# Rounding weight pieces on GpSimd instead of ScalarE, and copies ahead of an exponential, in a gated cross-attention and quantised FFN kernel

## The chip, the cores and the metric

The kernel runs on one core of a Trainium2 chip. The metric is the device time of one execution in microseconds (us). The engines are named PE (TensorE, matrix products), DVE (VectorE), ACT (ScalarE), POOL (GpSimd) and SP (SyncE, which here only starts transfers). Each engine takes its instructions in order, from its own queue.

## The reference

Two layers are computed one after the other, each added to its input through a tanh gate:

```python
x = x + tanh(g_xattn) * xattn(layernorm(x), ctx, Wq, bq, Wk, bk)
x = x + tanh(g_ffn)   * ffn(layernorm(x), w_gate, w_up, w_down)

def xattn(text, features, Wq, bq, Wk, bk):       # text, features (8, 256, 1024)
    Q = text @ Wq.T + bq
    K = features @ Wk.T + bk
    return softmax(Q @ K.T / sqrt(1024)) @ features

def fake_quant(t, axis):                         # one scale per row
    s = max(max(abs(t), axis) / 127, 1e-8)
    return clip(round(t / s), -128, 127) * s

def ffn(x, w_gate, w_up, w_down):                # 1024 -> 2752 -> 1024
    q = fake_quant
    h = silu(q(x) @ q(w_gate).T) * (q(x) @ q(w_up).T)
    return q(h) @ q(w_down).T
```

There are 8 batches of 256 tokens. The three FFN weights have to be quantised row by row: the largest magnitude of a row gives its scale, and each value is divided by the scale and rounded to a whole number.

## The kernel before

**Layout of the work.** The attention does not form Q and K. The kernel first multiplies the two attention weights into one matrix mt (lines 335 to 486), and the scores of a batch are then tokens x mt x features. After that a loop over the batches runs the attention (lines 645 to 695), and the FFN of all batches follows. The FFN weights are quantised during the mt product and the attention loop, in small portions between the attention's steps.

**Order.** From line 164 on to the first nine FFN products everything stands in the order in which the program text issues it ("manual_schedule"), so the text order is the order of each engine's queue. A tile pool with `bufs=n` gives n buffers for a tile's name; the next user of a buffer waits until the earlier user's readers are done.

**Weight pieces (lines 181 to 257).** `pieces` lists 92 portions of [128 rows x up to 1024 columns]: the row blocks of w_gate and w_up (44), and the row blocks of w_down in three column parts, first for the maximum (24) and then again for storing (24). `prepare()` makes one step of a pipeline over this list: it starts the load of piece i on SP (`prepare_load`), finishes piece i-3 (`prepare_store`), and scales piece i-2 (`prepare_scale`). Scaling is DVE's row maximum (L118) and inverse scale (L114), and then GpSimd's `raw * inv + MAGIC` in f32, in place (L209, L221 for w_down); adding MAGIC = 1.5 x 2^23 rounds to a whole number. Finishing is ScalarE's `raw - MAGIC` into the bf16 tile rq (L245, L234), and then a transfer: for w_gate and w_up a transposing DMA on SP into the resident weights (L246), for w_down a store to DRAM from ScalarE's queue (L240). `raw` has four buffers, `rq` has two. The last column part of w_down also gets 64 columns of zeros from ScalarE (L238).

**The attention loop.** Stage b does, in this order:

- `softmax_stage(b)` (L621): scores of the first token tile into a PSUM bank (L526); transposes of the next batch's normalised tokens by PE (L413), a quarter at a time, copied to xT by ScalarE (L436); DVE's shift nm (L534 to L536) and ScalarE's exponential (L542) of the first scores; the first half of the second tile's scores; quarters 2 and 3; one `prepare()`; the rest of the scores; the second shift and exponential.
- `tokens_bias` (L438): two row products on DVE (prod, L441), which write scratch tiles of the same pool name as xq (one buffer).
- `store_steps` (L593): ScalarE's rounding of a token tile of the batch before into xq (L596), and its store.
- eight query products (L508), each 16 matrix products that read all of xT, with ScalarE's copy to H (L512). Between them: transposes of the numerators with the copy pT (L548), the attention products (L555), the residual (L566, DVE, in place in xr), the stores of its rows to DRAM from GpSimd's queue (L667, L674), their statistics (L132), the root (L138, ScalarE, with a table load ahead of it) and inverse (L143 to L148), their normalisation in place (L151) and quantisation (L576), and the same statistics and normalisation for the tokens of the batch after next. `prepare()` stands ten times in a stage.

The token loads (xr, xn) and the feature loads are started on SP, in the same queue as the weight loads and the transposing DMAs.

Of the kernel before, what the change touches and what calls it, by code (L numbers as in the profile page):

```python
# [10 lines left out]
BF16 = mybir.dt.bfloat16  # L11
AF = mybir.ActivationFunctionType
ALU = mybir.AluOpType
# [4 lines left out]
P = 128  # L18


MAGIC = 12582912.0
# [6 lines left out]
def gated_xattn_ffn_kernel(  # L28
# [26 lines left out]
    nc = tc.nc  # L55
    B, S, D = x.shape
# [13 lines left out]
    def rows_of(c):  # L70
        return min(P, FF - c * P)
# [12 lines left out]
    nmagic = const.tile([P, 1], F32, name="nmagic")  # L84
# [15 lines left out]
    def chunk_of(name, c):  # L100
        if c == NFC - 1:
            return resident["tail"][:, :, :TAIL] if name == "wgT" else resident["tail"][:, :, TAIL:]
        t, c = (resident[name, 0], c) if c < CL else (resident[name, 1], c - CL)
        return t[:, :, c * P : (c + 1) * P]
# [5 lines left out]
    def scales(amax, s, tag="inv"):  # L110

        inv = small.tile(list(s.shape), F32, name="inv", tag=tag, bufs=3)
        nc.vector.tensor_scalar(s, amax, 1.0 / QMAX, SMIN, ALU.mult, ALU.max)
        nc.vector.reciprocal(inv, s)  # L114
        return inv

    def abs_max(dst, src):
        nc.vector.tensor_reduce(dst, src, AX.X, ALU.max, apply_absolute_value=True)  # L118
# [36 lines left out]
    def bank(tag):  # L155

        return psum.tile([P, HB], F32, name="ps_" + tag, tag=tag)
# [8 lines left out]
    if True:  # L166
        wraw = keep_scope.enter_context(tc.tile_pool(name="wraw", bufs=4, side=right))
# [13 lines left out]
        for c in range(NFC):  # L181
            pieces += [(w_gate, "wgT", swg, c), (w_up, "wuT", swu, c)]
            for r in range(c * KC // NFC, (c + 1) * KC // NFC):
                pieces += [(w_down, "max", i, r) for i in range(len(down_cols))]
                pieces += [(w_down, "store", i, r) for i in range(len(down_cols))]
        raws, downs = {}, {}
        step = [0]

        def prepare_load(i):
            src, kind, part, r = pieces[i]  # L190
            raws[i] = wraw.tile([P, D], F32, name="raw", tag="raw")
            if src is w_down:
                cols = down_cols[part]
                nc.sync.dma_start(
                    out=raws[i][:, : cols.stop - cols.start], in_=src[r * P : (r + 1) * P, cols]
                )
            else:
                n = rows_of(r)
                nc.sync.dma_start(out=raws[i][:n], in_=src[r * P : r * P + n, :])

        def prepare_scale(i):
            src, kind, part, r = pieces[i]
            raw = raws[i]
            if src is not w_down:
                n = rows_of(r)
                am = small.tile([P, 1], F32, name="wam", tag="wam")
                abs_max(am[:n], raw[:n])
                inv = scales(am[:n], part[:n, r : r + 1])
                nc.gpsimd.tensor_scalar(raw[:n], raw[:n], inv, MAGIC, ALU.mult, ALU.add)  # L209
                return  # L210
            w = down_cols[part].stop - down_cols[part].start
            if kind == "max":
                if part == 0:
                    downs[r] = small.tile([P, len(down_cols)], F32, name="dam", tag="dam")
                abs_max(downs[r][:, part : part + 1], raw[:, :w])
                if part == len(down_cols) - 1:
                    am = small.tile([P, 1], F32, name="wam", tag="wam")
                    nc.vector.tensor_reduce(am, downs[r], AX.X, ALU.max)
                    downs[r] = scales(am, swd[:, r : r + 1], "inv_d")
            else:  # L220
                nc.gpsimd.tensor_scalar(  # L221
                    raw[:, :w], raw[:, :w], downs[r], MAGIC, ALU.mult, ALU.add
                )

        def prepare_store(i):
            src, kind, part, r = pieces[i]
            raw = raws.pop(i)
            if kind == "max":
                return
            rq = wraw.tile([P, D], BF16, name="rq", tag="rq", bufs=2)  # L230
            if src is w_down:
                cols = down_cols[part]
                w = cols.stop - cols.start
                nc.scalar.activation(rq[:, :w], raw[:, :w], AF.Identity, bias=nmagic)  # L234
                if part == len(down_cols) - 1:

                    pad = NFC * P - FF
                    nc.scalar.activation(rq[:, w : w + pad], ones[:, :pad], AF.Identity, scale=0.0)  # L238
                    w += pad
                nc.scalar.dma_start(  # L240
                    out=wdq_dram[r][:, cols.start : cols.start + w], in_=rq[:, :w]
                )
            else:
                n = rows_of(r)
                nc.scalar.activation(rq[:n], raw[:n], AF.Identity, bias=nmagic[:n])  # L245
                nc.sync.dma_start_transpose(out=chunk_of(kind, r), in_=rq[:n])  # L246

        def prepare(n=1):
            for _ in range(n):
                i = step[0]  # L250
                if i < len(pieces):
                    prepare_load(i)
                if 0 <= i - 3 < len(pieces):
                    prepare_store(i - 3)
                if 0 <= i - 2 < len(pieces):
                    prepare_scale(i - 2)
                step[0] += 1
# [136 lines left out]
        for t in range(NTT):  # L394
            nc.sync.dma_start(
                out=x0[t], in_=x[0, t * P : (t + 1) * P, :].rearrange("p (c d) -> p c d", c=2)
# [13 lines left out]
        def transposes(src, blocks):  # L410
            pt = bank("tr").rearrange("p (i t) -> p i t", t=P)
            for i, k in enumerate(blocks):
                nc.tensor.transpose(pt[:, i, :], src[:, k * P : (k + 1) * P], ident)  # L413
            return pt
# [17 lines left out]
        def quarter_transposed(dst, src, g, copy):  # L432

            t, ks = g // 2, range(g % 2 * 4, g % 2 * 4 + 4)
            pt = transposes(src[t], ks)
            copy(dst[:, ks.start : ks.stop, t * P : (t + 1) * P], pt)  # L436
# [10 lines left out]
        cq = {}  # L447
# [76 lines left out]
        def scores(ps, t, js):  # L524
            for j in js:
                nc.tensor.matmul(  # L526
                    ps[:, :L], lhsT=H[:, j, t * P : (t + 1) * P], rhs=fT[:, j, :],
                    start=(j == 0), stop=(j == KC - 1),
                )

        def shift(ps, c):

            nm = small.tile([P, 1], F32, name="nm", tag="nm")
            nc.vector.tensor_reduce(nm, ps[:, :L], AX.X, ALU.max)  # L534
            nc.vector.tensor_scalar(nm, nm, c, -SCALE, ALU.add, ALU.mult)
            nc.vector.scalar_tensor_tensor(nm, c, SCALE, nm, ALU.mult, ALU.add)  # L536
            return nm

        def numerators(ps, nm):
            pe = work.tile([P, L], F32, name="pe", tag="pe")  # L540
            se = small.tile([P, 1], F32, name="se", tag="se")
            nc.scalar.activation(pe, ps[:, :L], AF.Exp, bias=nm, scale=SCALE, accum_out=se)  # L542
            return pe, se
# [77 lines left out]
        def softmax_stage(b, xn):  # L621

            nxt = b + 1 < B
            pss = [bank("s") for _ in range(NTT)]
            scores(pss[0], 0, range(KC))
            if nxt:
                quarter_transposed(xT, xn, 0, nc.scalar.copy)
                quarter_transposed(xT, xn, 1, nc.scalar.copy)
            nums = [numerators(pss[0], shift(pss[0], cq[b][:, 0:1]))]
            scores(pss[1], 1, range(KC // 2))  # L630
            if nxt:
                quarter_transposed(xT, xn, 2, nc.scalar.copy)
                quarter_transposed(xT, xn, 3, nc.scalar.copy)
                prepare()
            scores(pss[1], 1, range(KC // 2, KC))
            nums.append(numerators(pss[1], shift(pss[1], cq[b][:, 1:2])))
            return nums
# [6 lines left out]
        waiting = None  # L644
        for b in range(B - 1):
            nums = softmax_stage(b, xn)
            tokens_bias(b + 1, xn, scratch)
            if waiting:
# [224 lines left out]
    last = (B - 1) * NTT  # L873
    first = {"xq": load_quantised(0), "sx": sx01[:, 0:1, :], "h": []}
    nums = softmax_stage(B - 1, None)
    store_steps(*waiting)
    xr = load_tokens(B - 1, "xr")
    for r in range(KC):
        nc.sync.dma_start_transpose(
            out=wd_early[:, :, r * P : (r + 1) * P], in_=wdq_dram[r][:, : CA * P]  # L880
# [39 lines left out]
    for r in range(KC):  # L920
        nc.sync.dma_start_transpose(
            out=wd_late[:, :, r * P : (r + 1) * P], in_=wdq_dram[r][:, CA * P :]
# [59 lines left out]
    for i in range(2):  # L982
        cols = slice(i * HB // 2, (i + 1) * HB // 2)
# [44 lines left out]
```

## Time and profile before

| | us |
|---|---|
| three runs | 961.87, 964.85, 966.94 |
| their median | 964.85 |
| the profiled execution | 959.2 |
| its span | 957.1 |
| PE busy in it | 934.1 |
| DVE busy | 641.6 |
| ACT busy | 370.0 |
| POOL busy | 149.6 |
| granted PE clock | 1.00 |

The profile shows one execution. The span goes from the first to the last instruction; the profiled execution's own time is 2.1 us longer. Times in a timeline count from the start of the span. A group of instructions is named by its line in the kernel, its engine, its operation, and "out<-in" by tile names. "[1.83 <-ACT xT L436]" behind a row says that the engine had been idle for 1.83 us ahead of it, and that the idle time ended with a write of tile xT by ACT at line 436. In the list of waits the numbers are the total in us, how many times, and the longest. A softmax stage is named here by its b: stage 0 begins at 137 us in the trace, stage 6 at 418 us.

### The profile page before, as it was taken

What the parts mean: (1) busy time and instruction counts of PE and PEld (TensorE: products, weight loads), DVE (VectorE), ACT (ScalarE), POOL (GpSimd) and SP (SyncE); (2) the same over time, 40 slices, a digit from 0 to 9 for tenths busy, and PEclk for the clock granted to TensorE, in tenths of its full rate; (3) what the DMA queues carried; (4) which work ended last, traced back from release to release, by engine and by line L of the source; (5) the groups of instructions that cost most, each with busy time, mean ns of one, the idle gap of its engine ahead of it and who ended that gap; (6) DMA issues with size and microseconds to landing.
All of it is one profiled execution on the core that took longest, in us unless ns stands there. A gap on an engine that the chain in (4) does not pass through costs nothing.

```text
span 957.1 us, 14239 instructions
## 1 busy us (share of the span) xinstructions
PE 934.1 (98%) x5496; PEld 691.3 (72%) x5496; DVE 641.6 (67%) x1326; ACT 370.0 (39%) x660; POOL 149.6 (16%) x153
## 2 busy tenths in 40 slices
PE   9999999999999999999998899999999999999998
PEld 5444687868777878787877776858678586786854
DVE  5977825859585868686367757666576755767673
ACT  0022434445453536454537843423414143241420
POOL 0031311222221221122000003003030020302005
PEclk9999999999999999999999999999999999999999
DMA  9266876969698897967491512012120121201104
GB/s 349 91 170 201 217 237 171 310 214 265 223 241 283 212 288 202 263 208 236 135 204 49 107 23 76 13 23 90 23 89 1 23 89 23 89 1 47 44 1 154
DMA packets 125716, 135.95 MB, mean 142 GB/s; under 512 B 90256, under 2 KB 91536, under 8 KB 125648
## 3 DMA queue, kind: packets, MB, share of 16 engines
q1 hardware_dynamic: 112368, 104.36, 39.5%
q0 software_dynamic: 4784, 16.52, 4.5%
q10 hardware_dynamic: 8496, 14.16, 4.1%
q8 instruction: 43, 0.70, 0.3%
q14 instruction: 25, 0.20, 0.1%
HBM read 87.04 MB, written 26.74 MB: 119 GB/s over the span
## 4 chain that ended last, share of the span: by engine, by line
PE 80%; DVE 11%; ACT 5%; DMA 2%; issue 1%; POOL 0%; ACTq 0%; DVEq 0%
PE ps_g L748 14%; PE ps_tr L748 14%; PE ps_g L508 10%; PE ps_a L841 7%; PE ps_s L841 7%; PE ps_s L508 5%; PE ps_a L555 5%; PE ps_s L313 4%; PE ps_a L313 4%; PE ps_s L526 2%; PE ps_g L313 2%; PE ps_tr L413 2%; DMA wdq_dram<-rq 2%; DVE wam L118 2%; DVE st L132 1%
## 5 line engine op out<-in xcount | busy, mean ns | idle before, releaser
L508 PE MATMUL ps_g<-xT,mt 128*128 128x256 f32 x640 | 145.2, 380 | 4.5 <-ACT xT L436 4.5
L759 ACT ACTIVATE g<-g,swg 128x256 f32<-128x256 f32 (+1 forms) x176 | 79.7, 499 | 158.6 <-DVE g L757 158.6
L508 PEld LDWEIGHTS ps_g<-xT,mt 128*128 128x128 f32 x640 | 119.9, 190 | 25.1 <-ACT xT L436 6.7
L841 PEld LDWEIGHTS <-hq 128*128 128x128 bf16 x726 | 71.4, 98 | 76.0
L861 POOL TENSOR_TENSOR o<-o,xr 128x512 f32<-128x512 f32 x31 | 39.9, 1287 | 392.5 <-DVE o L858 385.5
L769 DVE SCALAR_TENSOR_TENSOR h<-ps_tr,swu,g 128x256 f32<-128x256 f32 x160 | 70.2, 482 | 43.5 <-ACT g L759 41.0
L209 POOL TENSOR_SCALAR raw<-raw,inv 128x1024 f32<-128x1024 f32 (+1 forms) x44 | 54.6, 1241 | 255.1 <-DVE inv L114 144.4
L748 PE MATMUL ps_tr<-xqb,wuT_lo 128*128 128x256 bf16 x704 | 84.7, 273 | 3.5 <-DVE h L769 3.5
L508 PE MATMUL ps_s<-xT,mt 128*128 128x256 f32 x384 | 86.9, 379 | 0.0
L783 DVE TENSOR_TENSOR acc<-acc,g 128x512 f32<-128x512 f32 (+2 forms) x88 | 56.4, 642 | 42.9 <-ACT g L773 42.1
L748 PE MATMUL ps_g<-xqb,wgT_lo 128*128 128x256 bf16 x704 | 84.7, 273 | 0.0
L748 PE MATMUL ps_tr<-xqb,wuT_hi 128*128 128x256 bf16 x640 | 77.7, 273 | 1.3 <-DVE h L769 1.1
L748 PE MATMUL ps_g<-xqb,wgT_hi 128*128 128x256 bf16 x640 | 77.7, 273 | 0.4 <-DVE g L757 0.4
L245 ACT ACTIVATE rq<-raw,nmagic 128x1024 bf16<-128x1024 f32 (+1 forms) x44 | 50.6, 1149 | 70.5 <-POOL raw L209 59.7
L508 PEld LDWEIGHTS ps_s<-xT,mt 128*128 128x128 f32 x384 | 71.2, 190 | 8.7
L748 PEld LDWEIGHTS <-wuT_lo 128*128 128x128 bf16 x704 | 68.9, 98 | 11.8 <-issue 3.8
L748 PEld LDWEIGHTS <-wgT_lo 128*128 128x128 bf16 x704 | 68.9, 98 | 9.9 <-issue 0.6
L826 DVE TENSOR_TENSOR h<-h,bc 128x512 f32<-128x512 f32 x80 | 51.7, 689 | 28.0 <-ACT bc L821 28.0
L748 PEld LDWEIGHTS <-wuT_hi 128*128 128x128 bf16 x640 | 62.6, 98 | 9.1 <-issue 1.8
L748 PEld LDWEIGHTS <-wgT_hi 128*128 128x128 bf16 x640 | 62.6, 98 | 8.0 <-issue 0.7
L566 DVE SCALAR_TENSOR_TENSOR xr<-ps_a,r,xr 128x512 f32<-128x512 f32 x32 | 23.9, 751 | 62.5 <-PE ps_a L555 62.5
L773 ACT ACTIVATE g<-h 128x512 f32<-128x512 f32 x72 | 45.2, 628 | 37.8 <-DVE h L769 37.8
(178 smaller groups left out, 1382.5 us busy)
## 6 DMA issues: line engine op xcount, KB each, us to landing
raw<-in_L_ffn_w_down_dram SPq DMA_DIRECT2D x32, 512.0 KB, 5.7
raw<-in_L_ffn_w_gate_dram SPq DMA_DIRECT2D x21, 512.0 KB, 4.7
raw<-in_L_ffn_w_up_dram SPq DMA_DIRECT2D x21, 512.0 KB, 5.5
fn<-in_ctx_dram SPq DMA_DIRECT2D x8, 1024.0 KB, 6.7
xr<-in_x_dram SPq DMA_DIRECT2D x16, 512.0 KB, 4.5
x_dram<-xr POOLq DMA_DIRECT2D x16, 512.0 KB, 5.2
xr<-x_dram SPq DMA_DIRECT2D x32, 256.0 KB, 3.4
out_dram<-o POOLq DMA_DIRECT2D x31, 256.0 KB, 3.7
```

What stands on the lines that cost most here:

```text
L209: nc.gpsimd.tensor_scalar(raw[:n], raw[:n], inv, MAGIC, ALU.mult, ALU.add)
L245: nc.scalar.activation(rq[:n], raw[:n], AF.Identity, bias=nmagic[:n])
L313: nc.tensor.matmul(pm, lhsT=a[:, c, k * P : (k + 1) * P], rhs=b[:, c, :], start=start, stop=stop)
L508: nc.tensor.matmul(ph, lhsT=mt[:, k, j * P : (j + 1) * P], rhs=xT[:, k, :], start=(k == 0), stop=(k == KC - 1),)
L555: nc.tensor.matmul(pas[h], lhsT=pT[:, l, :], rhs=f_tiles[b][:, l, halves[h]], start=(l == 0), stop=(l == NLT - 1),)
L748: nc.tensor.matmul(pb[:, i, :], lhsT=w[:, k, :], rhs=block["xq"][:, k, :], start=(k == 0), stop=(k == KC - 1),)
L759: nc.scalar.activation(g[:n, i, :], g[:n, i, :], AF.Silu, scale=swg[:n, c : c + 1])
L769: nc.vector.scalar_tensor_tensor(h[:n, i, :], src, swu[:n, c : c + 1], g[:n, i, :], ALU.mult, ALU.mult)
L773: nc.scalar.activation((acc if p == 0 else g)[:n, i, :], h[:n, i, :], AF.Abs)
L783: nc.vector.tensor_tensor(acc[:n, i, :], acc[:n, i, :], g[:n, i, :], ALU.max)
L826: nc.vector.tensor_tensor(h, h, ib.to_broadcast((P, 2, TB)), ALU.mult)
L841: nc.tensor.matmul(pds[t, half][:, cols], lhsT=hq[p][:, i, t * P : (t + 1) * P], rhs=wd[:, half * HB + cols.start : half * HB + cols.stop] ...
```

## The change

The rounding of a weight piece moves from `prepare_store` on ScalarE into `prepare_scale` on GpSimd, straight behind the scaling of the same piece, one step of the pipeline earlier; the bf16 tile rq is kept in a table until the next step stores it. The transfers stay where they were. In `softmax_stage` the exponential of the first token tile is issued behind the copies of quarters 2 and 3; its shift nm stays where it was on DVE.

```diff
@@ def prepare_scale(i):
                 inv = scales(am[:n], part[:n, r : r + 1])
-                nc.gpsimd.tensor_scalar(raw[:n], raw[:n], inv, MAGIC, ALU.mult, ALU.add)
+                rounded(i, raw[:n], inv)
                 return
...
             else:
-                nc.gpsimd.tensor_scalar(
-                    raw[:, :w], raw[:, :w], downs[r], MAGIC, ALU.mult, ALU.add
-                )
+                rounded(i, raw[:, :w], downs[r])
+
+        def rounded(i, raw, inv):
+            rows, cols = raw.shape
+            rq = wraw.tile([P, D], BF16, name="rq", tag="rq", bufs=2)
+            nc.gpsimd.tensor_scalar(raw, raw, inv, MAGIC, ALU.mult, ALU.add)
+            nc.gpsimd.tensor_scalar(rq[:rows, :cols], raw, MAGIC, None, ALU.subtract)
+            rqs[i] = rq
@@ def prepare_store(i):
-            raw = raws.pop(i)
             if kind == "max":
                 return
-            rq = wraw.tile([P, D], BF16, name="rq", tag="rq", bufs=2)
+            rq = rqs.pop(i)
             if src is w_down:
...
-                nc.scalar.activation(rq[:, :w], raw[:, :w], AF.Identity, bias=nmagic)
...
             else:
-                n = rows_of(r)
-                nc.scalar.activation(rq[:n], raw[:n], AF.Identity, bias=nmagic[:n])
-                nc.sync.dma_start_transpose(out=chunk_of(kind, r), in_=rq[:n])
+                nc.sync.dma_start_transpose(out=chunk_of(kind, r), in_=rq[: rows_of(r)])
@@ def softmax_stage(b, xn):
-            nums = [numerators(pss[0], shift(pss[0], cq[b][:, 0:1]))]
+            nm = shift(pss[0], cq[b][:, 0:1])
             scores(pss[1], 1, range(KC // 2))
             if nxt:
                 quarter_transposed(xT, xn, 2, nc.scalar.copy)
                 quarter_transposed(xT, xn, 3, nc.scalar.copy)
+            nums = [numerators(pss[0], nm)]
+            if nxt:
                 prepare()
```

More of the change, by code (lines that the diff above doesn't have):

```diff
@@ L185, in gated_xattn_ffn_kernel @@
                 pieces += [(w_down, "store", i, r) for i in range(len(down_cols))]
-        raws, downs = {}, {}
+        raws, rqs, downs = {}, {}, {}
         step = [0]
```

## The prediction

> **What bounds the kernel now.** I read the page first: busy time by engine, then the chain that ended last.
>
> ```profile
> PE 934.1 (98%) x5496; PEld 691.3 (72%) x5496; DVE 641.6 (67%) x1326; ACT 370.0 (39%) x660; POOL 149.6 (16%) x153
> ...
> PE 80%; DVE 11%; ACT 5%; DMA 2%; issue 1%; POOL 0%; ACTq 0%; DVEq 0%
> ```
>
> TensorE (PE) is busy for 934.1 of 957.1 us. Taking work off ScalarE (ACT, 39%) is worth nothing in itself; only the 23.0 us in which PE idles can be won. So I asked the waits of PE what ends this idleness.
>
> ```profile
> PE ps_g L508 <- ACT xT L436: 4.5, 5, 1.8
> ...
> PE ps_tr L413 <- ACT xT L436: 2.8, 2, 2.1
> ```
>
> Both are PE waiting for ScalarE's copies of the next tokens (xT). The other entries lie in the FFN part and at the ends, which the change does not touch. By windows of 20 us, 0.2 of the 4.5 falls at 107 us, ahead of the softmax stages. The rest, 7.1 us, belongs to five stages: 1.83 in b=1, 1.12 in b=2, 2.07 in b=3, 0.85 + 0.71 in b=4, 0.47 in b=5. Stages 0 and 6 have none. The timeline shows two causes. Stage 1:
>
> ```profile
> 190.71 4.07 POOL L221 TENSOR_SCALAR raw<-raw,inv 128x1024 f32<-128x1024 f32 x3 [14.80 <-DVE inv L114]
> ...
> 191.16 0.67 DVE L536 SCALAR_TENSOR_TENSOR nm<-cq,nm 128x1 f32<-128x1 f32 x1
> ...
> 191.87 0.47 ACT L542 ACTIVATE pe<-ps_s,nm 128x256 f32<-128x256 f32 x1 [3.10 <-DVE nm L536]
> ...
> 192.33 1.06 ACT L436 COPY xT<-ps_tr 128x512 f32<-128x512 f32 x2
> ...
> 192.96 3.72 PE L508 MATMUL ps_g<-xT,mt 128*128 128x256 f32 x16 [1.83 <-ACT xT L436]
> ...
> 194.10 1.75 DVE L441 SCALAR_TENSOR_TENSOR prod<-xn,v_bc 128x1024 bf16<-128x1024 f32 x1
> ...
> 195.90 1.15 ACT L596 ACTIVATE xq<-xr,nmagic 128x1024 bf16<-128x1024 f32 x1 [2.04 <-DVE prod L441]
> ...
> 197.85 0.36 ACT L548 COPY pT<-ps_tr 128x256 f32<-128x256 f32 x1
> ```
>
> The exponential waits for the shift nm, which VectorE (DVE) delivers late; two finished transposes queue behind it on ScalarE, and PE behind them. Stage 3 has the other cause:
>
> ```profile
> 281.86 1.54 POOL L209 TENSOR_SCALAR raw<-raw,inv 128x1024 f32<-128x1024 f32 x1 [3.72 <-issue]
> ...
> 283.43 1.15 ACT L245 ACTIVATE rq<-raw,nmagic 128x1024 bf16<-128x1024 f32 x1 [3.75 <-POOL raw L209]
> ...
> 284.49 1.05 ACT L436 COPY xT<-ps_tr 128x512 f32<-128x512 f32 x2
> ...
> 285.11 1.14 PE L413 MATMUL ps_tr<-ident,xn 128*128 128x128 f32 x8 [2.07 <-ACT xT L436]
> ```
>
> Here the rounding of a weight piece waits for GpSimd (POOL) and holds the first two copies.
>
> **The limit behind it.** In stage 1 the attention product after the next query product needs pT. On ScalarE that copy stands behind xq (L596), which waits for the second prod of VectorE. pT is ready at 197.85 + 0.36 = 198.21 and PE's weight load for the product starts at 199.98: slack 1.77. The same difference is 1.76 in stage 2, 1.30 in 3, 0.52 in 4, 0.51 in 5. VectorE is idle between the last residual (L566) and the prods only while it waits for the square root, so this is a serial chain. If D is how much it grows, a stage gains the smaller of its stall and (slack - D); below zero is a loss.
>
> **The change, part by part.**
>
> *Exponential behind the copies.* Nothing is added. Copies 2 and 3 need only their transposes, which end at 189.40 in stage 1: done by about 190.6, before PE ends its scores at 191.13. The table load (1.28 us, which ran while ScalarE waited) now follows them, to about 191.9, so the exponential runs where it ran before. Its user, the pe transposes behind 3.7 us of query product, has about 2 us to spare. This frees 1.83 + 1.12 + 0.85 + 0.47 = 4.3 us.
>
> *Rounding off ScalarE.* 44 instructions of 1149 ns (50.6 us) and 24 at L234 (18.3 + 7.0 us) leave it: 75.9 us, on an engine that is idle 61%. On the path that is 2.07 + 0.71 us, the stalls of stages 3 and 4. It also helps VectorE's chain:
>
> ```profile
> DVE rr L143 <- ACT rt L138: 9.3, 9, 2.7
> ```
>
> The root waits for a table load that starts after a rounding. With the rounding gone that load starts earlier, and the root is bounded by its input v or by the load: I read 0.4 + 0.7 saved in stage 1, 0.65 in 2, 1.2 in 3, 0.8 in 4, 1.2 in 5. ScalarE keeps the down-weight stores (L240) and the 8 pads (0.24 us each).
>
> *Rounding onto GpSimd.* 68 instructions. No row shows GpSimd writing bf16; the nearest is its scaling of the same tile, 1.12 us at the median. [...] GpSimd then holds about 150 + 68 x 1.12 = 226 us, no bound by itself. What costs is VectorE:
>
> ```profile
> 409.90 1.12 POOL L221 TENSOR_SCALAR raw<-raw,inv 128x1024 f32<-128x1024 f32 x1 [0.55 <-DMA raw<-in_L_ffn_w_down_dram]
> 410.00 1.56 DVE L576 TENSOR_SCALAR xr<-xr,inv 128x1024 f32<-128x1024 f32 x1
> ```
>
> L576 takes 0.753 at the median, so it was held 0.81 and let go at 410.81, 0.21 before GpSimd's recorded end. [...] I place each rounding behind its scaling and see what arrives in its 1.12 us, released 0.2 before its end as in the row:
>
> - Stage 1: nothing. The three scalings at 190.71 already run back to back, and the second prod (1.75 against 1.22) meets the third GpSimd instruction then as it will now. D = -1.1.
> - Stage 2: the root's small products L145 (0.5), L576 (0.16), less 0.65: D = 0.
> - Stage 3: L145 (0.5), L576 twice (0.2, 0.23), L151 of the next tokens (0.47), less 1.2: D = +0.2.
> - Stage 4: L576 twice, L151, and the second prod, as in stage 1 (0.53): 1.43 - 0.8, D = +0.63.
> - Stage 5: L151, L576, prod: 1.23 - 1.2, D = 0.
>
> Gains: 1.83; 1.12; min(2.07, 1.30 - 0.2) = 1.1; 0.52 - 0.63 = -0.1; min(0.47, 0.51) = 0.47. Sum 4.4 us. [...] I take the row, less 0.2 for the weight products at 104.8 (the second prod there, L441, can be held up to 0.8, ahead of mt rows that PE reads some 0.6 later), and less 0.9 for two further blocks of about 0.45 that I can't place. **3.3 us** faster.
>
> *Queues.* The store of a piece stays one step behind, the transposes on SP and the down stores on ScalarE. The rounding needs the rq buffer of two pieces earlier, so its transfer must have landed; that wait moves from ScalarE to GpSimd, one step earlier. Queued behind it there are the next scaling and the stores of the residual rows (L667, L674); VectorE's normalisation of those rows (L151, in place) waits for them. In stage 2 to 3 the store L667 was issued at 254.06. ScalarE's rounding there had waited for a landing until 256.92, so the worst new issue is 256.92 + 1.12 = 258.0; landing takes 5.7 at the median, 263.7, and L151 comes at 268.96: 5.2 us hide it. Without that cover each us late would be a us on VectorE's chain. SP no longer waits for ScalarE's rounding ahead of its transposes; loads are hidden either way (VectorE waits 1.8 us for raw in all), so I count 0.
>
> **The sum.** The profiled execution took 959.2 us, 2.1 beyond its span of 957.1; with 3.3 less it is 955.9. The runs shown have a median of 964.85, 5.65 above it, which I carry over: 964.85 - 3.3 = 961.5 us, 0.34% less.
>
> **The rivals.**
>
> 1. *All stalls go* (blocks on VectorE are fewer, or fall where it waits for PE): 7.1 us less, 957.8. For it: before each residual VectorE waits 2.9 to 5.7 us for PE. Against: those waits lie behind pT, not ahead of it, and stages 4 and 5 have a slack of only 0.5.
> 2. [...]
> 3. *The stall only changes its name*: PE waits for pT as long as it waited for xT, within 1 us of 964.85. For it: the same late VectorE releases both. Against: the slack of 1.77 in stages 1 and 2.
>
> **How the numbers follow.** Chances: forecast (1 to 4.8 us less) 0.42, rival 1 0.25, rival 2 0.20, rival 3 0.13. 0.5% is 4.8 us, about what a measurement of this kernel can tell from no change. Faster by more is rival 1: 0.25. Within it are forecast, rival 3 and a tenth of rival 2: 0.57. Slower by more: 0.18. The range goes from all stalls gone, 957.5, to 969, short of rival 2's 971.5; that leaves out about 2 in 10. The forecast's own range is 960 to 964.
>
> **What would show it.** PE's waits for xT should fall from 7.3 us to below 1. New PE waits for pT at L555 would be VectorE's chain, in stages 3 to 5 first. [...] The waits for the root should fall below 5 us. The forecast fails if PE waits for pT in stages 1 and 2, or if a residual store lands after its normalisation would start.

## The result, and the profile after

The changed kernel takes 963.46 us (median of 14 runs), against 963.57 us for the kernel before, measured beside it: a ratio of 0.9991, 95% interval 0.9972 to 1.0009. No change can be measured. The profiled execution took 961.49 us with a span of 959.4. A later comparison (e11, below) gave 0.9998 (0.9986 to 1.0011).

The page of the changed kernel: busy time by engine, and the chain that ended last.

```profile
PE 936.2 (98%) x5496; PEld 692.4 (72%) x5496; DVE 663.2 (69%) x1326; ACT 301.6 (31%) x592; POOL 338.0 (35%) x221
...
PE 76%; DVE 15%; ACT 5%; issue 2%; POOL 1%; DMA 1%; ACTq 0%; DVEq 0%; POOLq 0%
```

ScalarE lost 68 us. But GpSimd gained 188 where 76 were expected, and VectorE 21.6. VectorE's share of the last chain rose from 11% to 15%.

What PE waits for, after (lines have moved by one: the copy of xT is L437, the query product L509, the copy of pT L549, the attention product L556):

```profile
PE ps_a L556 <- ACT pT L549: 6.4, 4, 2.8
PE ps_g L509 <- ACT xT L437: 0.2, 1, 0.2
```

The waits for xT fell from 7.3 us to 0.2: the stalls the change aims at are gone. In their place stand 6.4 us of waits for pT, of which there were none: 2.2 in stage 3, 2.8 in stage 4, 1.0 in stage 5 and 0.4 in stage 6. The stall changed its name, and most of its place: stages 1 and 2 kept their gains, stages 3 to 6 lost them again.

The groups of instructions name the reason. They are the new rounding (L227) and the scaling (L226), with busy time, the mean of one in ns, and the idle time ahead of them:

```profile
L227 POOL TENSOR_SCALAR rq<-raw 128x1024 bf16<-128x1024 f32 (+2 forms) x68 | 188.9, 2778 | 30.6 <-DMA wdq_dram<-rq 20.0
...
L226 POOL TENSOR_SCALAR raw<-raw,inv 128x1024 f32<-128x1024 f32 (+2 forms) x68 | 82.8, 1218 | 148.2 <-DVE inv L114 92.8
```

Over the same 68 pieces the rounding takes 2.78 us in the mean and the scaling 1.22. The prediction had priced them alike. Stage 4 shows how a late GpSimd reaches PE (timeline after):

```profile
335.02 2.77 POOL L227 TENSOR_SCALAR rq<-raw 128x1024 bf16<-128x1024 f32 x1
...
337.77 1.65 POOL L226 TENSOR_SCALAR raw<-raw,inv 128x1024 f32<-128x1024 f32 x1
...
338.48 2.02 DVE L442 SCALAR_TENSOR_TENSOR prod<-xn,v_bc 128x1024 bf16<-128x1024 f32 x1
...
340.54 1.15 ACT L597 ACTIVATE xq<-xr,nmagic 128x1024 bf16<-128x1024 f32 x1 [2.65 <-DVE prod L442]
...
342.49 0.36 ACT L549 COPY pT<-ps_tr 128x256 f32<-128x256 f32 x1
...
342.91 3.70 PE L556 MATMUL ps_a<-fn,pT 128*128 128x512 f32 x8 [2.82 <-ACT pT L549]
```

The rounding of one piece runs until 337.79, so the scaling of the next starts only then, and lies across the second prod of VectorE: 2.02 us instead of 1.22. ScalarE's xq waits for that prod, the copy of pT stands behind xq, and PE waits 2.82 us for pT. (This stage shows the path, not yet the price: with a cheap rounding, in e7, it waits just as long.)

### The profile page after: what moved, and what is told of

It is laid out like the page before. It is cut to its first block, busy times and chain, and to the rows that moved or that the text cites. A ratio compares the mean times of both kernels' runs of the same rounds, so it can differ in the third digit from the quotient of the medians.

```text
span 959.4 us, 14231 instructions
## 1 busy us (share of the span) xinstructions
PE 936.2 (98%) x5496; PEld 692.4 (72%) x5496; DVE 663.2 (69%) x1326; ACT 301.6 (31%) x592; POOL 338.0 (35%) x221
## 4 chain that ended last, share of the span: by engine, by line
PE 76%; DVE 15%; ACT 5%; issue 2%; POOL 1%; DMA 1%; ACTq 0%; DVEq 0%; POOLq 0%
PE ps_g L751 13%; PE ps_tr L751 12%; PE ps_g L509 8%; PE ps_a L844 7%; PE ps_s L844 7%; PE ps_s L509 6%; PE ps_a L556 6%; PE ps_s L314 4%; PE ps_a L314 4%; PE ps_s L527 3%; PE ps_g L314 2%; DVE wam L118 2%; PE ps_tr L414 2%; DVE h L772 2%; DVE st L132 1%
## 5 line engine op out<-in xcount | busy, mean ns | idle before, releaser
L227 POOL TENSOR_SCALAR rq<-raw 128x1024 bf16<-128x1024 f32 (+2 forms) x68 | 188.9, 2778 | 30.6 <-DMA wdq_dram<-rq 20.0
L509 PE MATMUL ps_g<-xT,mt 128*128 128x256 f32 x640 | 144.9, 379 | 0.3 <-ACT xT L437 0.2
L226 POOL TENSOR_SCALAR raw<-raw,inv 128x1024 f32<-128x1024 f32 (+2 forms) x68 | 82.8, 1218 | 148.2 <-DVE inv L114 92.8
L509 PEld LDWEIGHTS ps_g<-xT,mt 128*128 128x128 f32 x640 | 120.2, 190 | 19.5 <-issue 3.3
L509 PE MATMUL ps_s<-xT,mt 128*128 128x256 f32 x384 | 86.9, 379 | 0.0
L509 PEld LDWEIGHTS ps_s<-xT,mt 128*128 128x128 f32 x384 | 71.2, 190 | 8.7
L556 PE MATMUL ps_a<-fn,pT 128*128 128x512 f32 x128 | 59.7, 610 | 6.4 <-ACT pT L549 6.4
```

The source lines that it names most:

```text
L226: nc.gpsimd.tensor_scalar(raw, raw, inv, MAGIC, ALU.mult, ALU.add)
L227: nc.gpsimd.tensor_scalar(rq[:rows, :cols], raw, MAGIC, None, ALU.subtract)
L509: nc.tensor.matmul(ph, lhsT=mt[:, k, j * P : (j + 1) * P], rhs=xT[:, k, :], start=(k == 0), stop=(k == KC - 1),)
L556: nc.tensor.matmul(pas[h], lhsT=pT[:, l, :], rhs=f_tiles[b][:, l, halves[h]], start=(l == 0), stop=(l == NLT - 1),)
```

## The experiments

**Theory A**, after the result: PE's waits for pT come from VectorE's chain, which GpSimd makes later, and pT is hit only because its copy stands behind xq on ScalarE. Rivals: the exponential's new place makes them; or pT itself is not what matters.

**e1: the exponential alone.** The second edit of the change, with the rounding left on ScalarE.

```diff
-            nums = [numerators(pss[0], shift(pss[0], cq[b][:, 0:1]))]
+            nm = shift(pss[0], cq[b][:, 0:1])
...
+            nums = [numerators(pss[0], nm)]
```

> Only the second part of the change: the first exponential behind the copies of quarters 2 and 3, rounding still on ScalarE. Theory A (the changed kernel lost what the reorder won because the rounding on GpSimd lengthens VectorE's chain to pT): the reorder alone wins, per stage the smaller of its stall and the slack of pT, 1.77 + 1.12 in stages 1 and 2, 0.52 + 0.47 in 4 and 5, so 3.9 us less than before; the stalls of 2.07 and 0.71 behind a rounding on ScalarE stay. Theory B (PE would have waited for pT as long as for xT in any case, whoever rounds): within 1 us of before.

957.51 us, ratio 0.9935 (0.9915 to 0.9954): 4.4 to 8.2 us faster, more than the 3.9 expected. This edit alone is a gain, and the other one spends it. PE still waits 2.8 us for xT (stages 3 and 4, ScalarE's rounding) and 1.8 for pT. From the first to the last attention product the profile shows 335.3 us against 338.2 before, 2.9 less. The profiled execution, 958.61 us, was the longest of its six runs, so it shows only a part of the gain.

**e2: the rounding alone.** The first edit, with the exponential in its old place.

```diff
-            nm = shift(pss[0], cq[b][:, 0:1])
+            nums = [numerators(pss[0], shift(pss[0], cq[b][:, 0:1]))]
...
-            nums = [numerators(pss[0], nm)]
```

> Only the first part: rounding on GpSimd, the exponential in its old place. Theory A: the 2.8 us of stalls behind a rounding on ScalarE go, the 4.3 us behind the exponential stay and grow with VectorE's lateness (1.4, 1.8 and 1.0 us more in stages 3 to 5, read from the changed kernel), so 1 to 3 us slower than before. Theory B: 2.8 us less than before.

971.93 us, ratio 1.0086 (1.0065 to 1.0107): 8.3 us slower, far more than expected. The waits of PE:

```profile
PE ps_g L509 <- ACT xT L437: 13.6, 7, 3.9
```

With the exponential ahead of the copies, every us that VectorE is late holds xT, and 13.6 us of waits is nearly twice what the kernel before has. So the two edits interact. By PE's waits for xT and pT the exponential's new place frees 7.0 us on top of the GpSimd rounding (13.6 to 6.6) and 2.5 us alone (7.3 to 4.8). The ratios point the same way (1.0086 to 0.9991, against 1 to 0.9935), but their intervals leave a difference of this size open.

**e3, e4, e6: the copy of pT ahead of xq.** One edit (it takes ScalarE's copy to H of the first query product ahead of xq as well), on top of the changed kernel (e3), of e1 (e4), and of the kernel before (e6):

```diff
+            queries_between(0)
+            pT = numerators_transposed(nums[0][0])
             if waiting:
                 store_steps(*waiting)
-            queries_between(0)
             xr = load_tokens(b, "xr")
-            pT = numerators_transposed(nums[0][0])
```

> The changed kernel with the copy pT ahead of xq on ScalarE (the store of the earlier token tile stands behind the numerators' transpose, and the next token loads behind that), so pT no longer waits for VectorE's prods. Theory A: PE's waits for pT (6.4 us) go, 6 to 7 us less than before, near 957. Theory B (something else makes pT late, ScalarE's own work or PE): waits for pT stay above 4 us and the time stays within 2 us of before.

> The reorder of the exponential with pT ahead of xq, rounding on ScalarE as before. Theory A: the full 4.3 us of stalls behind the exponential go and the 2.8 us behind a rounding on ScalarE stay: 4.3 us less than before, 0.4 less than the reorder alone. If it equals or beats the same order with rounding on GpSimd, that rounding brings nothing; theory A expects it 2 to 3 us behind that one.

> The kernel before with only pT ahead of xq on ScalarE; exponential and rounding as before. Theory A: PE waits for xT there, not for pT, so nothing changes, within 1 us of before. Theory C (the order of pT and xq alone is what wins): 4 us or more less than before.

e3: 954.18 us, ratio 0.9899 (0.9878 to 0.9920), 9.7 us faster than before, where 6 to 7 were expected; no wait for pT is left, and one of 1.6 us for fT is new. e4: 956.19 us, 0.9924 (0.9904 to 0.9943), 5.5 to 9.2 us faster where 4.3 were expected; only the 2.8 us behind ScalarE's rounding are left. (Freed waits give back more than their own length; two reasons are shown under e8 and in the last section.) e6: 963.12 us, 1.0011 (1.0000 to 1.0022), no gain, with 5.8 + 2.8 us of waits for xT. So the pT copy behind xq is how the loss reaches PE, and it matters only once the exponential no longer holds xT. Theory A stands on how the loss reaches PE; it does not say why VectorE became so late.

**e5: what the rounding costs by itself.** Theory 2: the form of the instruction, one subtraction, costs 2.8 us. Rivals: the bf16 output costs it, or VectorE's work beside it stretches it. Twelve GpSimd instructions on 128x1024 tiles were added at the start of the kernel before, ahead of the work on the weights:

```diff
+        for _ in range(2):
+            nc.gpsimd.tensor_scalar(pg, pf, MAGIC, None, ALU.subtract)
+            nc.gpsimd.tensor_scalar(ph16, pf, MAGIC, None, ALU.subtract)
+            nc.gpsimd.tensor_scalar(pg, pf, 2.0, MAGIC, ALU.mult, ALU.add)
+            nc.gpsimd.tensor_scalar(ph16, pf, 2.0, MAGIC, ALU.mult, ALU.add)
+            nc.gpsimd.tensor_scalar(ph16, pi16, MAGIC, None, ALU.subtract)
+            nc.gpsimd.tensor_copy(ph16, pf)
```

> The kernel before with twelve GpSimd instructions of 128x1024 added at its start, six forms twice, whose results nothing reads: one subtraction f32 to f32, the same f32 to bf16, multiplication and addition f32 to f32, the same f32 to bf16, one subtraction bf16 to bf16, and a copy f32 to bf16. Theory 1: the bf16 output makes the rounding's 2.77 us (f32 outputs 1.1, all bf16 outputs about 2.8). Theory 2: the single subtraction form does (2.8 for both outputs, 1.1 for multiplication and addition with either). [...]

The timeline of e5, GpSimd alone, first round, in the diff's order (start, duration):

```profile
3.04 2.78 POOL L180 TENSOR_SCALAR pg<-pf 128x1024 f32<-128x1024 f32 x1
5.80 2.92 POOL L181 TENSOR_SCALAR ph<-pf 128x1024 bf16<-128x1024 f32 x1
8.70 1.47 POOL L182 TENSOR_SCALAR pg<-pf 128x1024 f32<-128x1024 f32 x1
10.13 1.47 POOL L183 TENSOR_SCALAR ph<-pf 128x1024 bf16<-128x1024 f32 x1
11.69 3.08 POOL L184 TENSOR_SCALAR ph<-pi 128x1024 bf16<-128x1024 bf16 x1
14.83 1.04 POOL L185 CAST ph<-pf 128x1024 bf16<-128x1024 f32 x1
```

The f32 subtraction (2.78) costs as much as the one into bf16 (2.92), and product-and-sum into bf16 (1.47) as much as into f32. The output type is not it. Nor is it VectorE: the first row ran for 2.1 of its 2.78 us before VectorE began its own work at 5.18. Later rows ran beside VectorE, and differ between the rounds: in the second the same six took 3.21, 2.79, 1.04, 1.47, 3.08 and 1.57 us.

**e10: the operation or the number of operations.** Six other forms in the same place:

```diff
+            nc.gpsimd.tensor_scalar(pg, pf, MAGIC, None, ALU.add)
+            nc.gpsimd.tensor_scalar(pg, pf, 2.0, None, ALU.mult)
+            nc.gpsimd.tensor_scalar(pg, pf, 1.0, MAGIC, ALU.mult, ALU.subtract)
+            nc.gpsimd.tensor_scalar(pg, pf, MAGIC, 1.0, ALU.subtract, ALU.mult)
+            nc.gpsimd.tensor_scalar(pg, pf, MAGIC, MAGIC, ALU.add, ALU.subtract)
+            nc.gpsimd.tensor_scalar(ph16, pf, 1.0, -MAGIC, ALU.mult, ALU.add)
```

> The kernel before with two times six GpSimd instructions on 128x1024 tiles added at its start, in this order: single sum f32 to f32; single product f32 to f32; product then subtraction f32 to f32; subtraction then product f32 to f32; sum then subtraction f32 to f32; product then sum f32 to bf16. If the subtraction is what costs, the third, fourth and fifth read about 2.8 us and the others 1.0 to 1.5. If the missing second operation costs, the first two read 2.8 and the other four 1.0 to 1.5. If only product then sum is fast, all but the last read 2.8.

```profile
20.85 3.19 POOL L178 TENSOR_SCALAR pg<-pf 128x1024 f32<-128x1024 f32 x1
24.13 2.77 POOL L179 TENSOR_SCALAR pg<-pf 128x1024 f32<-128x1024 f32 x1
26.98 4.07 POOL L180 TENSOR_SCALAR pg<-pf 128x1024 f32<-128x1024 f32 x1
31.13 3.89 POOL L181 TENSOR_SCALAR pg<-pf 128x1024 f32<-128x1024 f32 x1
35.10 4.11 POOL L182 TENSOR_SCALAR pg<-pf 128x1024 f32<-128x1024 f32 x1
39.19 1.36 POOL L183 TENSOR_SCALAR ph<-pf 128x1024 bf16<-128x1024 f32 x1
```

This is the second round of e10. In the first, a single sum took 2.79 us, all of it ahead of VectorE's work. A single sum or product costs what the single subtraction does (2.8 to 3.2), the three other pairs cost still more (3.6 to 4.1 over both rounds), and only product then sum is fast (1.36, and 1.53 in the first round). The scaling's 1.12 us, the row that the prediction took its price from, belongs to that one pair.

**e7, e11, e12: the changed kernel with the cheap form.** `raw * 1.0 + (-MAGIC)` gives the same values as `raw - MAGIC`. This tests the rest of the prediction, since its price of 1.12 us then holds:

```diff
-            nc.gpsimd.tensor_scalar(rq[:rows, :cols], raw, MAGIC, None, ALU.subtract)
+            nc.gpsimd.tensor_scalar(rq[:rows, :cols], raw, 1.0, -MAGIC, ALU.mult, ALU.add)
```

> The changed kernel, with the GpSimd rounding written as a product with 1.0 and a sum with minus MAGIC in one instruction, which computes the same values, in place of a single subtraction. Theory 2 (the form of the instruction costs 2.77 us, and the rest of the prediction holds): the rounding reads about 1.1 us at 128x1024, GpSimd falls from 338 to about 226 us busy, PE's waits for pT from 6.4 to under 2.5 us, and the kernel is 3.3 us faster than before (2.7 to 4.4), ratio 0.996 to 0.997. Rival (each further GpSimd instruction holds VectorE once, whatever its length): the waits for pT stay above 4 us and the time within 1 us of before, ratio 0.999 to 1.001.

959.16 us, ratio 0.9965 (0.9953 to 0.9977): 3.4 us faster than before (2.2 to 4.5), where the recorded forecast said 3.3. In the profile of e7:

```profile
L227 POOL TENSOR_SCALAR rq<-raw 128x1024 bf16<-128x1024 f32 (+2 forms) x68 | 74.1, 1090 | 60.3 <-DMA wdq_dram<-rq 51.0
```

and, from its waits:

```profile
PE ps_a L556 <- ACT pT L549: 4.5, 2, 2.9
```

The rounding reads 1.09 us and GpSimd 223.8 us, where the prediction's sum gave 226. But 4.5 us of waits for pT remain (1.60 in stage 3, 2.88 in stage 4), and under 2.5 was expected; that part missed, and waits above 4 us were the sign of the rival, by which each further GpSimd instruction holds VectorE once, whatever its length. In stage 4 of e7 it is the cheap rounding that lies across the second prod:

```profile
334.28 1.96 POOL L227 TENSOR_SCALAR rq<-raw 128x1024 bf16<-128x1024 f32 x1
...
335.38 1.93 DVE L442 SCALAR_TENSOR_TENSOR prod<-xn,v_bc 128x1024 bf16<-128x1024 f32 x1
```

So the price makes the waits of stages 5 and 6 and a part of stage 3's, and the place on GpSimd makes that of stage 4 (0.29 us in e1, with the rounding on ScalarE). The two kernels were then put on one chip, since their first comparisons had been made apart:

> The changed kernel unaltered, beside the next run on one chip. The first comparison gave 0.9991 [0.9972, 1.0009] and PE's waits for pT 6.4 us. Theory 2 and its rival both expect 0.998 to 1.001 here; they differ in the step from this run to the next.

> The changed kernel with the rounding as product and sum, on the same chip as the run before. Theory 2: 2 to 3.5 us faster than the changed kernel there (ratios to before apart by 0.002 to 0.0036), waits for pT 4.5 us. Rival (the gap between the two forms came from different chips): less than 1 us apart.

e11, the changed kernel unaltered: 962.18 us, ratio 0.9998 (0.9986 to 1.0011), waits for pT 7.3 us. e12, the cheap form: 959.39 us, 0.9966 (0.9954 to 0.9978), waits 4.3. The intervals are apart; the form alone is worth about 3 us.

**e9: the rounding alone, in the cheap form.** The edit of e7 on e2.

> The rounding on GpSimd alone (the exponential in its old place), in the form with two operations. With the single subtraction this was 8.3 us slower than before, with 13.6 us of PE's waits for xT. Theory 2: the stalls of stages 1 and 2 stay (1.83 and 1.12), those of stages 3 and 4 go in part, so that PE waits 3 to 5.5 us for xT and the time is from 3 us below to 1 us above before. Rival (the place on GpSimd, not the price, makes the loss): 4 us or more slower, waits for xT above 9 us.

964.19 us, ratio 1.0015 (1.0005 to 1.0025), with 8.7 us of waits for xT where 3 to 5.5 were expected. Against e2 (1.0086) the form saves 6.8 us. What is left, 1.4 us slower than before, lies a little beyond theory 2's end of 1 us: even cheap, this edit alone gains nothing. That the holds on VectorE eat up what ScalarE's freed queue brings fits this, but no run separates the two.

**e8: cheap form and pT first.** The edit of e7 on e3, the best version found.

> As the run before, with ScalarE's copy of pT also put ahead of xq. Theory 2: VectorE's chain is then shorter as well as off PE's path; PE idles as little as with the pT copy first and the slow rounding (20.3 us), and the time is 0.9895 of before or below by up to 1.5 us. Rival (the order on ScalarE already takes out every stall that VectorE's chain could cause): no difference to the slow rounding, ratio 0.990 within 0.002.

952.25 us, ratio 0.9896 (0.9874 to 0.9917): 10.0 us faster than before. Its interval nearly coincides with that of e3 (0.9878 to 0.9920), as the rival said: with pT first, the time no longer shows what the rounding costs. A difference of up to 3 us, theory 2's 1.5 among them, would not show between these intervals. From its page, the chain that ended last:

```profile
PE 91%; DMA 3%; DVE 2%; ACT 2%; issue 1%; SPq 0%; ACTq 0%; DVEq 0%
```

VectorE's 15% of the changed kernel is now 2% (in e3 it is 11%). Between the first and the last attention product PE idles 1.5 us (329.0 less 327.5 busy), against 8.6 before: all 7.1 us of the stalls that the prediction listed. In e3 it idles 5.2 us there. 2.3 of these stand at 416 us: ScalarE had been idle for 8.01 us behind a store that waits for the rounding L227. So the rounding can still reach PE by another way; that execution was 4.1 us longer than e3's median.

The other 2.1 us of the 338.2 - 329.0 = 9.2 are a shorter busy time of PE itself (329.6 before), and they belong to the waits too. The records of products in a row overlap by 0.16 us; a product behind a wait has no such overlap, and its record is up to 0.10 us longer. In stage 1, from the start of the scores' row at 189.24 to the transposes behind the query product at 196.52, the kernel before takes 7.28 us, and e8 5.18 (189.58 to 194.76): 2.10 less, for a wait of 1.83. Eight products differ in this way, by 2.0 us together.

## Why the prediction was right or wrong

The time, 963.46 us, lies 2 us above the forecast of 961.5 and inside its range, and no measurable change had the highest chance. But the forecast was a gain of 3.3 us, and e11's interval (1.3 us faster to 1.1 slower) excludes it. That the time lies even within the forecast's own 960 to 964 is luck: it counted from 964.85, a median of three runs, and the kernel before, measured beside the change, had 963.57; from there that range ends at 962.6. By its number what took place is rival 3, the stall that only changes its name, to which the text gave 0.13; by its mechanism only in part, since stages 1 and 2 kept their gains, and about 3 us of the loss are the price of the rounding (e11 and e12).

- **What bounds the kernel, and the stalls freed: right.** PE's waits for xT fell to 0.2 (below 1 was said). Stages 1 and 2 gained their 1.83 and 1.12, and e8 shows that all 7.1 us were there to be had.
- **The limit behind it: right.** The waits for pT appeared at the line named, in stages 3 to 5 first. e3 and e6 show the mechanism.
- **The rounding's price: the step that failed.** The sum's 68 x 1.12 gives the rounding the time of the scaling's row. But the two are not the same form: the scaling is a product and a sum, the rounding one subtraction. It measured 2.78 us in the mean, and GpSimd's total 338 us instead of 226. The mechanism was right; this term of the sum was mis-sized. With the form that has the assumed price (1.09 us in e7), e7 and e12 measure 3.4 and 3.3 us less than before.
- **D, the growth of VectorE's chain: too small in stages 3 and 4, even at the right price.** In e7 the gain of stage 3 is 2.07 - 1.60 = 0.5, so D = 1.30 - 0.5 = 0.8 (0.2 was said); in stage 4 it is 1.56 - 2.88 = -1.3, so D = 1.8 (0.63 was said). Stages 1, 2 and 5 show no stall, as predicted. By the waits e7 gains 7.1 - 4.5 = 2.6 where the stages' sum was 4.4; the 1.1 us taken off for blocks that could not be placed covered most of the error. So the agreement of 3.4 with 3.3 is in part luck. In the changed kernel D is 1.4, 1.8 and 1.0 in stages 3, 4 and 5, and the waits sum to a gain of 7.1 - 6.4 = 0.7.
- **Which VectorE work is held.** The prediction listed L145, L576, L151 and the prods. They make 11.4 of the 21.6 us by which VectorE's busy time grew (L151 5.4, L576 3.2, prods 2.0, L145 0.8); the longest of L151 went from 0.81 to 1.60 us, the longest prod from 1.75 to 2.02. No row before shows a hold of L151 (all 30 of its instructions take 0.79 to 0.81 us there), so its terms in the stages' D were the author's estimate. But the line that grew most is not in the list, and neither is the third: the small two-column operations L148, the last step of the inverse root, and L446, the last step of the token bias. L148: minimum, median and maximum in ns, of the changed kernel:

```profile
L148 DVE TENSOR_SCALAR rstd<-rr x16: 168/560/1002, 96.2 to 504.3; 128x2 f32<-128x2 f32 x16
```

and of e7:

```profile
L148 DVE TENSOR_SCALAR rstd<-rr x16: 168/169/944, 95.3 to 501.1; 128x2 f32<-128x2 f32 x16
```

With the slow form more of these are held (median 560 against 169), but none for much longer. L148 makes 6.0 us of the growth (16 of 547 ns instead of 170) and L446 4.1 (8 of 736 instead of 229). In e7 VectorE's busy time still grew by 12.1 us, 3.4 of it L148.

The remaining points:

- **The root: right by stage, but for stage 4, and nearly so as a total.** The waits of the first root of a stage fell by 0.4, 0.66, 1.2, 0.51 and 1.05 us in the five places where 0.4, 0.65, 1.2, 0.8 and 1.2 were said. The second root of stage 1 lost its 0.7 as said. The total of 9.3, counted from 147 to 465 us, fell to 5.5 in the same window, where below 5 was said; one root, at 417.48, waits longer (1.65 instead of 0.83).
- **Rival 2, slower in every stage (971.5 us)**, did not come about: stages 1 and 2 show no wait for pT. **The residual stores** did no harm: the one that was bounded at 258.0 was issued at 258.73, in a trace that ran 1.0 us later from stage 0 on, and landed at 262.2; the normalisation L151 follows at 266.0 and shows no idle time for it.
- **The carried difference** of 5.65 us between median and profiled run was too large as a constant: the kernel before had medians of 961.47 to 962.95 in the later comparisons. The runs say what most of it is. The profiled run had a mean granted clock of 1.000. Of the 34 runs of the kernel before beside e7, two had 1.000 (959.8 us in the mean), eleven 0.998 (962.0) and eighteen 0.996 (963.9). The last section shows where the clock is lost.

## What to carry to other kernels

Price a moved operation by a row of the same engine and the same pair of operations, not only the same tile; where there is none, the range has to be wide, and rewriting `x - c` as `x * 1.0 + (-c)` costs no accuracy here and made the instruction 2.5 times as fast (1.09 us instead of 2.78). When a stall is removed, look at what is next in the same in-order queue: here the copy of pT ahead of xq was worth 9 us on the changed kernel, 1 us on e1 (within the noise), and nothing on the kernel before, where the exponential stood ahead of it. Where two edits come together, run each alone: one gained 6 us, the other lost 8. And count a long stall of PE dearer than its length: one of 2.18 us cost 1.7 us more by the clock, those of up to 2.1 us in the softmax stages nothing more (next section).

## What the runs showed of the hardware that was not expected

**Of the arithmetic forms tried, one is fast on GpSimd.** At 128x1024 f32: product then sum 1.04 to 1.53 us, copy into bf16 1.04 to 1.57, the single operations tried 2.77 to 3.21, the three other pairs 3.64 to 4.11. Why is not shown.

**The slow form held VectorE twice, with a gap between.** In stage 3 of the changed kernel:

```profile
275.87 2.80 POOL L227 TENSOR_SCALAR rq<-raw 128x1024 bf16<-128x1024 f32 x1
...
276.02 0.91 DVE L148 TENSOR_SCALAR rstd<-rr 128x2 f32<-128x2 f32 x1
276.96 0.81 DVE L151 TENSOR_SCALAR xn<-xn,mv,rstd 128x1024 f32<-128x1024 f32 x1
277.69 1.52 DVE L151 TENSOR_SCALAR xn<-xn,mv,rstd 128x1024 f32<-128x1024 f32 x1
```

L148, 0.17 us of work, is let go some 0.9 us after the rounding's start. The first normalisation then runs unhindered for 0.81 us inside the rounding. The second takes 1.52 us, so it was held until about 278.4, some 0.25 us before the rounding's end. In the late part not all work is held: in stage 4 the first prod, which reads two tiles, starts at 337.21, 0.6 us before the end of a rounding, and takes its usual 1.22 us. The longest prod is 2.02 us in both kernels, with the slow form and with the fast. The prediction's row of the fast form (409.90, kernel before) shows one hold, which ended 0.21 us ahead of the scaling's end; the rows of the slow form show two holds and 0.9 us of free passage between them. GpSimd loses time beside VectorE too: the scaling at 337.77, which starts 0.66 us ahead of the end of a prod (337.21 + 1.22), takes 1.65 us instead of 1.12.

**A wait of PE cost 1.7 us more by the clock; where it falls decides.** The traces record a granted clock of either 1.00 or 0.50. While PE works, each stretch of 0.50 lasts 3.41 us, and those of one execution lie whole multiples of 3.41 us apart (in the changed kernel they begin at 293.45 and 959.05, 195 times 3.413 apart). Here is the changed kernel in windows of this length, in step with its slow stretch, around the stalls of stages 3 and 4 (PE busy, weight loads, VectorE, ScalarE, GpSimd, then the granted clock):

```profile
290.04:293.45 3.41, 1.23 (x5) 0.59 (x4) 2.09 (x9) 2.26 (x4) 1.22 (x2) 1.00 0.55 154
293.45:296.86 3.41, 3.41 (x6) 1.33 (x5) 0.75 (x1) 0.00 (x0) 2.67 (x1) 0.50 0.99 398
...
337.82:341.23 3.41, 2.27 (x11) 1.66 (x9) 3.34 (x5) 0.76 (x2) 3.32 (x2) 1.00 0.64 100
341.23:344.65 3.42, 1.74 (x4) 0.87 (x5) 1.58 (x4) 1.56 (x4) 1.89 (x1) 1.00 0.71 222
344.65:348.06 3.41, 3.41 (x14) 2.17 (x13) 2.16 (x3) 0.37 (x1) 0.36 (x1) 1.00 1.14 305
```

and the row of stage 3's attention products:

```profile
292.77 5.40 PE L556 MATMUL ps_a<-fn,pT 128*128 128x512 f32 x8 [2.18 <-ACT pT L549]
```

The wait of 2.18 us in stage 3 lies in one window, and the next window has half the clock: the eight products take 5.40 us, and the same eight 3.70 in stage 4, so the wait cost another 1.7. The wait of stage 4 is longer, 2.82 us, but a window's edge parts it into 1.15 and 1.67, and the clock stays. All profiles taken, cut in this way from 20 us on, have 3832 windows. Each of the 18 in which PE idles 2.18 us or more is followed by half clock; of two with 1.98 one is; of the others, with less, none. So of the thirteen waits of 2.18 us and more in the softmax stages nine were followed by a slow stretch, and the four others (2.49, 2.73, 2.82 and 3.18) were parted by an edge. The 21 waits of 1.0 to 2.1 us had none.

The stall of 2.18 us in stage 3 thus cost 3.9 us, more than two of 1.1 without a slow stretch, which no term of the prediction held: between the first and the last attention product the changed kernel idles 0.4 us less than before (8.2 against 8.6) and its PE is busy 1.0 us longer (330.6 against 329.6). In the window ahead of the slow stretch PE was idle for 2.18 of the 3.41 us and busy for 1.23. Why the clock falls is not shown.
